# Moving two subtract/add steps from VectorE to GpSimd, and one projection in place of two, in a four-layer scan network

## The chip, the cores and the metric

The kernel runs on one NeuronCore of a Trainium2 chip. The metric is the device time of one launch in microseconds. Three runs of the kernel before gave 19587.28, 19610.84 and 19634.19 us, so the median is 19610.84 us. The engines are called as in the profile: PE (TensorE, matmuls), DVE (VectorE), ACT (ScalarE), POOL (GpSimd), and SP, which issues the DMAs. Each engine works through its own instructions in order; semaphores make one engine wait for another.

## The reference

The input is four images of 64 x 64 tokens with 96 channels, in float32. Four layers follow, each with a mixer and a feed-forward part, both with a residual. The mixer of layer 0 is a small gated recurrence. The mixers of layers 1 to 3 are selective scans over the image in four directions (row order and column order, each forward and backward), with 192 inner channels and 16 states. Cut to what matters:

```python
xz = x_norm @ in_proj_w.T;  xc, z = split(xz)          # 192 + 192
xc = silu(depthwise_conv3x3(xc) + conv_b)
xs = stack([rows, columns, flip(rows), flip(columns)]) # 4 directions
x_dbl = einsum('bkdl,kcd->bkcl', xs, x_proj_weight)    # 6 + 16 + 16 rows
dts, B, C = split(x_dbl, [6, 22])
delta = softplus(dt_w @ dts + dt_bias)
h = exp(delta * A) * h + (delta * u) * B               # along 4096 tokens
y = sum_n(h * C) + D * u
out = (layernorm(sum of directions of y) * silu(z)) @ out_proj_w.T
x = x + out
t = x + ffn(layernorm(x))      # ffn on float8-rounded values
```

The line that gives `dts`, `B` and `C` from `x_dbl`, and the residual `x = x + out`, are the two places that the change touches.

## The kernel before, in words

**Stages.** First comes `gated`, layer 0 of all images. Then `scans` runs twelve stages, one for each image of layers 1, 2 and 3. At the end the feed-forward part of the last image is left over and runs alone.

**The scan.** A stage is 2 directions of time x 4 segments of 1024 tokens x 3 channel chunks x 16 states = 384 tiles, so 4608 tiles in all. One tile is 128 partitions x 1024 tokens: two halves of 64 channels in row and column order. For tile `k`, with its state `n`:

- `c_rows`: SP reads two rows of C from a DRAM buffer `cs`, each spread over 64 partitions, into `c` (6 buffers), two tiles ahead
- `decays`: ACT makes `da = exp(delta * A)` (3 buffers), two tiles ahead
- `b_rows`: PE spreads a row of B over 128 partitions of PSUM with a selecting matmul, into `bc` (2 buffers), one tile ahead
- `scan`: DVE multiplies `bc` by `du`, then runs the recurrence into `h` (3 buffers)
- `times_c`: POOL multiplies `h` by `c`, for the tile before
- `accumulate`: PE adds `h * c` to `acc` in PSUM, for the tile three before

**Work beside the scan.** Everything else is written as Python generators that `yield` between steps. Between the multiply and the recurrence of each tile the function `beside` takes one step of `chain` (`prepare_chunk`: `delta` and `du` of the next 16 tiles), one step of `segment` (`prepare_segment`: the projections of the next 48 tiles), and some steps of a `Job`. A `Job` is the work between two mixers of one image: `join_orders`, `mixer_out`, `feed_forward`, `take_in`, `convolve`, eight strips of 512 tokens each. It earns `rate` steps a tile (1.65 for most jobs). A step is only taken when one of two PSUM banks (`bank`, `release`) is free where it needs one. The order thus written out in Python is the order on each engine, since the class `InOrder` chains the instructions of an engine. All its calls have one line in the profile, L78.

**B in three parts.** The selecting matmul works in bf16, and B is held as a sum of three bf16 numbers in the 96 partitions of `bs`: the rounded value, the rounded remainder, and the remainder of that. `prepare_segment` gets B in three copies (partitions 0 to 95) and `dts` (12 partitions) from one projection, `x_proj_b`, per half segment. ACT copies `dts` into `rows` and the rounded B into `bs`; DVE subtracts `bs` from the PSUM copy of B, into `rows`; ACT copies this to two thirds of `bs`; POOL makes the last subtraction. A second projection, `x_proj_c`, then gives the 32 rows of C, which ACT copies into `rows` and SP writes to `cs`.

**The residual.** `mixer_out` ends a strip with the projection `out_proj` into PSUM; DVE adds it to the strip `xr` of x, giving `x1` (tile `x`). One step later DVE takes the layer norm's statistics of `x1` (`measure`: `bn_stats` into `st`, `bn_aggr` into `mv`).

Of the kernel before, what the change touches and what calls it, by code (L numbers as in the profile page):

```python
# [15 lines left out]
ALU = mybir.AluOpType  # L16
# [4 lines left out]
C = 96  # L21
NS = 16
DI = 192
R = 6
HID = 4 * C
T = 1024
MM = 512
G = MM // 128
# [8 lines left out]

NB3 = 96
NC2 = 2 * NS
XPW = NB3 + 2 * R + NC2  # L40
W_IN = 0
W_OUT = W_IN + 6 * 128
W_CW = W_OUT + 2 * C
# [5 lines left out]
W_XP = W_LN + 4  # L49
W_SSM = W_XP + 6 * XPW  # L50

# [48 lines left out]
def metaformer(ctx: ExitStack, tc: tile.TileContext, x, l0_ab, l0_rest, ssm, ffn, out):  # L100
    nc = tc.nc
    pe, act, dve, pool, sp = (
        InOrder(tc, e) for e in (nc.tensor, nc.scalar, nc.vector, nc.gpsimd, nc.sync)
    )
# [6 lines left out]
    def sb(bufs, tag, shape, dtype=F32):  # L111
        return pools[bufs].tile(shape, dtype, tag=tag, name=tag)

    def const(name, shape, dtype=F32):
        return pools[1].tile(shape, dtype, name=name)
# [9 lines left out]
    def bank(name):  # L125
        banks["free"] -= 1
        return banks["pool"].tile([128, MM], F32, tag="ps", name=name)

    def release():
        banks["back"] += 1  # L130
# [31 lines left out]
    for k in range(2):  # L162
        p = slice(64 * k, 64 * k + 64)
# [31 lines left out]
    for layer in range(4):  # L195
# [8 lines left out]
        b = const(f"b_{layer}", [128, 3 + C])  # L204
# [72 lines left out]
    class Weights:  # L277
# [17 lines left out]
        def load_xp(self):  # L295
            if self.xp is None:
                self.xp = sb(1, "xp", [128, 6 * XPW])
                sp.dma_start(out=self.xp, in_=ssm[self.layer - 1, :, W_XP:W_SSM])
# [57 lines left out]
    def mixer_out(im, layer, s, hold):  # L356

        w = weights[layer].w
        yt, norm = hold.pop(("y", s))
        zl, zh, xr = load_z(im, s)  # L360
        yield from norm.settle()
        yield
        normalise(yt, yt, DI, norm.r, norm.nm)
        yield
        yield True
        g = []
        for i, (a, b, z) in enumerate(((0, 128, zl), (128, 192, zh))):
            ps = bank("y_c")
            transpose_strip(ps, yt, a, b)
            yield  # L370
            v = sb(1, f"u{i}", [128, MM])
            m = b - a
            sc, bias = (w[0:m, W_LN + 2 * i + k : W_LN + 2 * i + k + 1] for k in range(2))
            act.activation(v[0:m], ps[0:m], AF.Identity, bias=bias, scale=sc)
            release()
            yield i == 0
            g.append(v)
            if i == 0:
                continue
            for v, z, m in ((g[0], zl, 128), (g[1], zh, 64)):  # L380
                pool.tensor_tensor(v[0:m], v[0:m], z[0:m], ALU.mult)
                yield
        yield True
        ps = bank("out_proj")
        for q in range(G):
            t = slice(128 * q, 128 * q + 128)
            o = ps[:, C * q : C * q + C]
            pe.matmul(o, g[0][:, t], w[:, W_OUT : W_OUT + C], start=True, stop=False)
            pe.matmul(o, g[1][0:64, t], w[0:64, W_OUT + C : W_OUT + 2 * C], start=False, stop=True)
            yield  # L390
        yield
        x1 = sb(2, "x1", [128, G, C])
        dve.tensor_tensor(x1, xr, ps[:, 0 : G * C].rearrange("p (g c) -> p g c", g=G), ALU.add)
        release()
        yield
        norm = Norm()
        yield from norm.measure(x1, C, 1e-5)
        hold["x", s] = x1, norm
# [376 lines left out]
    def prepare_segment(item, sg):  # L775

        xp = weights[item.layer].xp
        m = NB3 + 2 * R

        def project(ps, a, b, k):  # L780

            for c in range(3):
                o = (3 * item.d + c) * XPW
                cols = slice(k * MM, (k + 1) * MM)
                pe.matmul(
                    ps[0 : b - a],
                    xp[:, o + a : o + b],
                    sg.us[c][:, cols],
                    start=c == 0,
                    stop=c == 2,  # L790
                )
                if c:
                    yield

        sg.rows = sb(1, "rows", [128, T])
        for k in range(2):
            cols = slice(k * MM, (k + 1) * MM)
            ps = bank("x_proj_b")
            yield from project(ps, 0, m, k)

            bs = sg.bs[:, cols]
            act.copy(sg.rows[NB3:m, cols], ps[NB3:m])
            sg.steps = k == 1
            act.copy(bs, ps[0:NB3])
            yield
            rem = sg.rows[0:NB3, cols]
            dve.tensor_tensor(rem, ps[0:NB3], bs, ALU.subtract)
            release()
            yield
            for p in (32, 64):  # L810
                act.copy(bs[p : p + 32], rem[p : p + 32])
            yield k == 0
        pool.tensor_tensor(sg.bs[64:96], sg.rows[64:96], sg.bs[64:96], ALU.subtract)
        for k in range(2):
            cols = slice(k * MM, (k + 1) * MM)
            yield True
            ps = bank("x_proj_c")
            yield from project(ps, m, m + NC2, k)
            act.copy(sg.rows[0:NC2, cols], ps[0:NC2])
            release()  # L820
        yield
        sp.dma_start(out=sg.cs, in_=sg.rows[0:NC2])

    def prepare_chunk(item):

# [481 lines left out]
    with tc.tile_pool(name="pbig", bufs=2, space=bass.MemoryType.PSUM) as wides_pool:  # L1307
        wides.append(wides_pool)
        with tc.tile_pool(name="pl0", bufs=1, space=bass.MemoryType.PSUM) as pl0:
            gated(images, Job(between(images[0], 0), 2.6, patience=1), pl0)  # L1310
        stages = [(im, layer) for layer in range(1, 4) for im in images]
        jobs = []
        for at in range(len(stages)):
            jobs.append([])
            if at + 1 < len(stages):
                im, layer = stages[at + 1]
                jobs[-1].append(Job(between(im, layer - 1), 1.65))

            for im in {10: images[:2], 11: images[2:3]}.get(at, ()):
                jobs[-1].append(Job(between(im, 3, im.dst), 2.6))  # L1320
        with tc.tile_pool(name="pac", bufs=1, space=bass.MemoryType.PSUM) as pac:
            scans(stages, jobs, pac)
# [38 lines left out]
def _scan(in_w, conv_w, conv_b, xp_w, dt_w, dt_b, A_logs, Ds, ln_w, ln_b, out_w):  # L1361
    w = np.zeros((128, W_SSM), np.float32)
    twice = np.r_[128:DI, 128:DI]

    xp = np.zeros((128, 2, 3, XPW), np.float32)
    m = NB3 + 2 * R
    for d in range(2):
        for chunk, halves in enumerate(CHUNKS):
            for k, (ch, order) in enumerate(halves):
                t = xp_w[2 * d + order].T[ch : ch + 64]  # L1370
                v = xp[64 * k : 64 * k + 64, d, chunk]
                for s in range(3):
                    v[:, 32 * s + NS * order : 32 * s + NS * order + NS] = t[:, R : R + NS]
                v[:, NB3 + R * order : NB3 + R * order + R] = t[:, :R]
                v[:, m + NS * order : m + NS * order + NS] = t[:, R + NS :]
    w[:, W_XP:W_SSM] = xp.reshape(128, -1)
    t = in_w.T
    w[:C, W_IN : W_IN + 448] = np.concatenate([t[:, :128], t[:, twice], t[:, DI:]], 1)
    dt = np.zeros((2 * R, 2, 3, 128), np.float32)
    for d in range(2):  # L1380
        for chunk, halves in enumerate(CHUNKS):
            for k, (ch, order) in enumerate(halves):
                t = dt_w[2 * d + order].T
                dt[R * order : R * order + R, d, chunk, 64 * k : 64 * k + 64] = t[:, ch : ch + 64]
    w[NB3 : NB3 + 2 * R, W_IN:W_OUT] = dt.reshape(2 * R, -1)
    w[:, W_OUT : W_OUT + C] = out_w.T[:128]
    w[:64, W_OUT + C : W_CW] = out_w.T[128:]
    taps = conv_w.reshape(DI, 9)
    w[:, W_CW : W_CW + 9] = taps[:128]
    w[:64, W_CW + 9 : W_CB] = np.concatenate([taps[128:, 0:3], taps[128:, 6:9]], 1)  # L1390
    w[64:, W_CW + 9 : W_CW + 12] = taps[128:, 3:6]
    w[:, W_CB:W_DTB] = np.stack([conv_b[:128], conv_b[twice]], 1)
    w[:, W_DTB:W_AL] = _chunks(dt_b[..., None]).reshape(128, -1)
    w[:, W_AL:W_DS] = _chunks(A_logs.reshape(4, DI, NS)).reshape(128, -1)
    w[:, W_DS:W_LN] = _chunks(Ds.reshape(4, DI, 1)).reshape(128, -1)
    w[:, W_LN : W_LN + 2] = np.stack([ln_w[:128], ln_b[:128]], 1)
    w[:64, W_LN + 2 : W_XP] = np.stack([ln_w[128:], ln_b[128:]], 1)
    return w
# [46 lines left out]
```

## Time and profile before

| what | value |
|---|---|
| median of the runs | 19610.84 us |
| time of the profiled execution | 19605.71 us |
| its span on the core | 19603.9 us |
| granted TensorE clock, mean | 0.816 |
| ACT busy | 62% of the span |
| DMA engines, queue q1 | 61.6% of their span |
| ACT table loads | 1165, 1494.7 us |

A page of the profile shows the busy time of each engine and the costliest groups of instructions. A group's line has the engine, the operation, the tiles written and read (out<-in), the shape, the count, the busy time and the mean duration of one, and after a bar the time that the engine stood idle just before these instructions, with what ended it. A list of waits sums the same idle time by who waited for whom. Waits under 150 ns are not put down to anyone.

### The profile page before, as it was taken

Reading aid. Unit: us, or ns where it says so; the run is one execution under the profiler, and the core shown is the slowest. Engines: PE = TensorE matmul, PEld = TensorE weight load, DVE = VectorE, ACT = ScalarE, POOL = GpSimd, SP = SyncE. Lnnn points to the kernel's source line nnn. Section 1 sums busy time; section 2 is a strip of 40 time slices with the busy share of each in tenths; the row PEclk is TensorE's granted clock in tenths of the full one; section 3 lists DMA queues with packets and bytes.
Section 4 is the critical chain, followed back from the end, with each engine's and each line's share of the span. In section 5 each row is a group of like instructions: output and inputs, shape, how many; then the busy total and the mean of one; then the engine's idle time right before and its main releaser. Section 6 shows DMA issues by size and latency. Waiting matters only on the chain. (4 is left out here: it accounts for less than half of the span.)

```text
span 19603.9 us, 224830 instructions
## 1 busy us (share of the span) xinstructions
PE 16279.3 (83%) x70400; PEld 4745.4 (24%) x70400; DVE 17669.3 (90%) x13768; ACT 12248.8 (62%) x19341; POOL 15496.4 (79%) x10086
## 2 busy tenths in 40 slices
PE   8998787787888888887888887887888888888877
PEld 3332121121122222222222222222222222223223
DVE  6757999999999999999999999999999999998885
ACT  4544665665665665675665665665675665666665
POOL 3435888888888888888888888888888888888886
PEclk9998786787787787797797797797797797797776
DMA  2213666676666666667666667666666666676664
GB/s 52 50 47 89 166 184 168 168 188 166 169 186 172 170 182 180 167 185 182 169 183 180 167 182 183 167 182 182 168 186 178 168 185 176 171 185 171 168 177 115
DMA packets 1269876, 3192.65 MB, mean 163 GB/s; under 512 B 440336, under 2 KB 440560, under 8 KB 1262544
## 3 DMA queue, kind: packets, MB, share of 16 engines
q1 hardware_dynamic: 1268688, 3178.27, 61.6%
q8 instruction: 568, 9.31, 0.2%
q14 instruction: 620, 5.08, 0.1%
HBM read 2818.81 MB, written 308.28 MB: 160 GB/s over the span
## 5 line engine op out<-in xcount | busy, mean ns | idle before, releaser
L78 POOL TENSOR_TENSOR c<-h,c 128x1024 f32<-128x1024 f32 (+1 forms) x4992 | 11332.9, 2276 | 3284.9 <-DVE h L78 1396.4
L78 DVE TENSOR_TENSOR_SCAN h<-da,carry,bc 128x1024 f32<-128x1024 f32 x4608 | 10797.5, 2343 | 598.7 <-POOL c L78 80.8
L78 PE MATMUL acc<-c,twice 64*64 64x512 f32 x36864 | 6246.6, 755 | 57.4 <-POOL c L78 57.4
L78 ACT ACTIVATE da<-delta,decay 128x1024 f32<-128x1024 f32 x4608 | 5280.8, 1148 | 1372.5 <-DVE h L78 1359.7
L78 DVE TENSOR_TENSOR bc<-du,bc 128x1024 f32<-128x1024 f32 x4608 | 5567.1, 1208 | 417.8 <-PE bc L78 389.6
L78 PE MATMUL bc<-bs,sel 96*128 96x512 bf16 x9216 | 3398.6, 457 | 2393.3 <-DVE h L78 2296.6
L78 ACT COPY carry<-h 128x1 f32<-128x1 f32 x3456 | 649.1, 188 | 2997.7 <-DVE h L78 2992.8
L78 PEld LDWEIGHTS <-sel 96*128 96x128 bf16 x9216 | 557.0, 101 | 7376.4 <-DVE h L78 5607.2
L78 PEld LDWEIGHTS acc<-c,twice 64*64 64x64 f32 x36864 | 1131.3, 153 | 2848.4 <-issue 1927.6
L78 ACT ACT_TABLE_LOAD x1165 | 1494.7, 1283 | 36.3 <-DVE mv L78 20.0
L78 PE MATMUL conv<-pad,tap_lo 128*128 128x512 f32 x1728 | 913.5, 639 | 0.6 <-ACT zh L78 0.6
L78 PE MATMUL dt_proj<-rows,w 12*128 12x512 f32 x1152 | 829.5, 807 | 6.3 <-ACT delta L78 6.3
L78 ACT ACTIVATE du<-e,ones 128x1024 f32<-128x1024 f32 x576 | 659.4, 1145 | 202.9 <-POOL delta L78 197.8
L78 POOL TENSOR_TENSOR delta<-delta,du 128x1024 f32<-128x1024 f32 x288 | 679.2, 2358 | 121.7 <-ACT du L78 121.3
L78 PE MATMUL x_proj_c<-u,xp 128*32 128x512 f32 x1152 | 657.8, 687 | 133.2 <-ACT rows L78 125.0
L78 PE MATMUL x_proj_b<-u,xp 128*108 128x512 f32 x1152 | 696.1, 722 | 53.7 <-ACT u L78 12.8
L78 ACT COPY y<-acc 128x1024 f32<-128x1024 f32 x288 | 291.3, 1012 | 713.8 <-PE acc L78 708.9
L78 POOL TENSOR_TENSOR e<-e,du 128x1024 f32<-128x1024 f32 x288 | 679.7, 2360 | 2.4 <-ACT du L78 2.4
L78 POOL TENSOR_TENSOR du<-delta,u 128x1024 f32<-128x1024 f32 x288 | 680.0, 2361 | 0.1
L78 POOL TENSOR_TENSOR delta<-delta,e 128x1024 f32<-128x1024 f32 x288 | 678.7, 2357 | 0.1
L78 ACT ACTIVATE c<-c,l_bias 128x512 f32<-128x512 f32 x384 | 263.6, 686 | 662.6 <-PE c L78 659.8
L78 PE MATMUL conv<-pad,tap_hi 128*128 128x512 f32 (+1 forms) x1152 | 598.8, 621 | 3.8 <-ACT u L78 3.8
(152 smaller groups left out, 15323.9 us busy)
## 6 DMA issues: line engine op xcount, KB each, us to landing
c<-cs SPq DMA_DIRECT2D x9216, 256.0 KB, 4.2
u<-u SPq DMA_DIRECT2D x288, 512.0 KB, 6.8
y<-y SPq DMA_DIRECT2D x1152, 128.0 KB, 3.5
y<-y SPq DMA_DIRECT2D x144, 512.0 KB, 6.4
xr<-x SPq DMA_DIRECT2D x224, 192.0 KB, 5.1
u<-u SPq DMA_DIRECT2D x288, 128.0 KB, 2.7
pad<-y SPq DMA_DIRECT2D x288, 128.0 KB, 5.1
z<-zl SPq DMA_DIRECT2D x96, 256.0 KB, 3.4
```

The costliest lines, as they stand in the source:

```text
L78: ins = f(*a, **k).ins
```

## The change

1. `prepare_segment` has one projection in place of two, over 108 output rows in a new order: B once (0 to 31), C (32 to 63), B again (64 to 95), `dts` (96 to 107). The weight columns of `xp` are laid out for it. `x_proj_c` and its copies are gone.
2. ACT copies all 108 rows into `rows`, and B rounded to bf16 into `bs[0:32]`. The first subtraction of B's parts runs on POOL, on 32 partitions, from `rows` and `bs`, both in SBUF. ACT's two copies to `bs` follow two steps later. The write of C to `cs` comes right after them, ahead of POOL's last subtraction.
3. In `mixer_out` ACT copies `out_proj` out of PSUM into `x1`, one step later POOL adds `xr` to it, and two steps after that the statistics begin.
4. Most jobs have the rate 1.62 in place of 1.65.

```diff
-XPW = NB3 + 2 * R + NC2
+XPW = NB3 + 2 * R
...
         x1 = sb(2, "x1", [128, G, C])
-        dve.tensor_tensor(x1, xr, ps[:, 0 : G * C].rearrange("p (g c) -> p g c", g=G), ALU.add)
+        act.copy(x1, ps[:, 0 : G * C].rearrange("p (g c) -> p g c", g=G))
         release()
+        yield
+        pool.tensor_tensor(x1, x1, xr, ALU.add)
+        yield
         yield
         norm = Norm()
...
     def prepare_segment(item, sg):
         xp = weights[item.layer].xp
+        rows = sg.rows = sb(1, "rows", [128, T])
+        for k in range(2):
+            cols = slice(k * MM, (k + 1) * MM)
+            ps = bank("x_proj")
             for c in range(3):
                 o = (3 * item.d + c) * XPW
                 pe.matmul(
+                    ps[0:XPW], xp[:, o : o + XPW], sg.us[c][:, cols], start=c == 0, stop=c == 2
                 )
                 if c:
                     yield
             bs = sg.bs[:, cols]
-            act.copy(sg.rows[NB3:m, cols], ps[NB3:m])
+            act.copy(rows[0:XPW, cols], ps[0:XPW])
             sg.steps = k == 1
-            act.copy(bs, ps[0:NB3])
-            yield
-            rem = sg.rows[0:NB3, cols]
-            dve.tensor_tensor(rem, ps[0:NB3], bs, ALU.subtract)
+            act.copy(bs[0:32], ps[0:32])
             release()
             yield
+            rem = rows[64:96, cols]
+            pool.tensor_tensor(rem, rows[0:32, cols], bs[0:32], ALU.subtract)
+            yield
+            yield
             for p in (32, 64):
-                act.copy(bs[p : p + 32], rem[p : p + 32])
+                act.copy(bs[p : p + 32], rem)
             yield k == 0
-        pool.tensor_tensor(sg.bs[64:96], sg.rows[64:96], sg.bs[64:96], ALU.subtract)
-        for k in range(2):
-            cols = slice(k * MM, (k + 1) * MM)
-            yield True
-            ps = bank("x_proj_c")
-            yield from project(ps, m, m + NC2, k)
-            act.copy(sg.rows[0:NC2, cols], ps[0:NC2])
-            release()
-        yield
-        sp.dma_start(out=sg.cs, in_=sg.rows[0:NC2])
+        sp.dma_start(out=sg.cs, in_=rows[NC2 : 2 * NC2])
+        pool.tensor_tensor(sg.bs[64:96], rows[64:96], sg.bs[64:96], ALU.subtract)
...
-                jobs[-1].append(Job(between(im, layer - 1), 1.65))
+                jobs[-1].append(Job(between(im, layer - 1), 1.62))
```

More of the change, by code (lines that the diff above doesn't have):

```diff
@@ L777, in prepare_segment @@
         xp = weights[item.layer].xp
-        m = NB3 + 2 * R
-        def project(ps, a, b, k):
+        rows = sg.rows = sb(1, "rows", [128, T])
+        for k in range(2):
+            cols = slice(k * MM, (k + 1) * MM)
+            ps = bank("x_proj")
             for c in range(3):
                 o = (3 * item.d + c) * XPW
-                cols = slice(k * MM, (k + 1) * MM)
                 pe.matmul(
[L786 to L790, printed above, removed]
+                    ps[0:XPW], xp[:, o : o + XPW], sg.us[c][:, cols], start=c == 0, stop=c == 2
                 )
@@ L793, in project @@
                     yield
-        sg.rows = sb(1, "rows", [128, T])
-        for k in range(2):
-            cols = slice(k * MM, (k + 1) * MM)
-            ps = bank("x_proj_b")
-            yield from project(ps, 0, m, k)
             bs = sg.bs[:, cols]
-            act.copy(sg.rows[NB3:m, cols], ps[NB3:m])
+            act.copy(rows[0:XPW, cols], ps[0:XPW])
             sg.steps = k == 1
-            act.copy(bs, ps[0:NB3])
-            yield
-            rem = sg.rows[0:NB3, cols]
-            dve.tensor_tensor(rem, ps[0:NB3], bs, ALU.subtract)
+            act.copy(bs[0:32], ps[0:32])
             release()
             yield
+            rem = rows[64:96, cols]
+            pool.tensor_tensor(rem, rows[0:32, cols], bs[0:32], ALU.subtract)
+            yield
+            yield
             for p in (32, 64):
-                act.copy(bs[p : p + 32], rem[p : p + 32])
+                act.copy(bs[p : p + 32], rem)
             yield k == 0
-        pool.tensor_tensor(sg.bs[64:96], sg.rows[64:96], sg.bs[64:96], ALU.subtract)
-        for k in range(2):
-            cols = slice(k * MM, (k + 1) * MM)
-            yield True
-            ps = bank("x_proj_c")
-            yield from project(ps, m, m + NC2, k)
-            act.copy(sg.rows[0:NC2, cols], ps[0:NC2])
-            release()
-        yield
-        sp.dma_start(out=sg.cs, in_=sg.rows[0:NC2])
+        sp.dma_start(out=sg.cs, in_=rows[NC2 : 2 * NC2])
+        pool.tensor_tensor(sg.bs[64:96], rows[64:96], sg.bs[64:96], ALU.subtract)
     def prepare_chunk(item):
@@ L1365, in _scan @@
     xp = np.zeros((128, 2, 3, XPW), np.float32)
-    m = NB3 + 2 * R
     for d in range(2):
@@ L1371, in _scan @@
                 v = xp[64 * k : 64 * k + 64, d, chunk]
-                for s in range(3):
-                    v[:, 32 * s + NS * order : 32 * s + NS * order + NS] = t[:, R : R + NS]
+                v[:, NS * order : NS * order + NS] = t[:, R : R + NS]
+                v[:, NC2 + NS * order : NC2 + NS * order + NS] = t[:, R + NS :]
                 v[:, NB3 + R * order : NB3 + R * order + R] = t[:, :R]
-                v[:, m + NS * order : m + NS * order + NS] = t[:, R + NS :]
     w[:, W_XP:W_SSM] = xp.reshape(128, -1)
```

## The prediction

> **What bounds the kernel now.** I read the busy times first, then the same by stretch. In a stretch's row come its length, then each engine's busy time.
>
> ```profile
> PE 16279.3 (83%) x70400; PEld 4745.4 (24%) x70400; DVE 17669.3 (90%) x13768; ACT 12248.8 (62%) x19341; POOL 15496.4 (79%) x10086
> ```
> ```profile
> core 0: us, PE busy (x) PEld busy (x) DVE busy (x) ACT busy (x) POOL busy (x), PEclk, DMA share, GB/s
> ...
> 2700.00:18900.00 16200.00, 13428.88 (x60392) 3721.43 (x60390) 15179.46 (x10951) 10425.05 (x15995) 13570.31 (x8024) 0.81 0.67 176
> ```
>
> The scans fill 1804 to 19388 us. In their middle DVE is busy 15179 of 16200 us (94%), POOL 84%, PE 83%. DVE is the bound, with 1021 us of gaps. The groups of instructions by shape price DVE's work, removed rows last:
>
> ```profile
> L78 DVE TENSOR_TENSOR_SCAN h<-da,carry,bc 128x1024 f32<-128x1024 f32 x4608 | 10797.5, 2343 | 598.7 <-POOL c L78 80.8 <-ACT norm L78 20.7 <-ACT da L78 5.4
> L78 DVE TENSOR_TENSOR bc<-du,bc 128x1024 f32<-128x1024 f32 x4608 | 5567.1, 1208 | 417.8 <-PE bc L78 389.6 <-POOL carry L78 23.3 <-PE ff_xt L78 2.7
> L78 DVE TENSOR_TENSOR rows<-x_proj_b,bs 96x512 f32<-96x512 f32 x192 | 130.1, 677 | 45.5 <-ACT bs L78 45.3
> L78 DVE TENSOR_TENSOR x<-xr,out_proj 128x384 f32<-128x384 f32 x96 | 52.6, 548 | 70.9 <-PE out_proj L78 46.6 <-issue 14.7 <-POOL hq L78 9.2
> ```
>
> The change takes 130.1 + 52.6 = 182.7 us of busy time off DVE. The timeline of DVE shows that this is not the gain (start, duration):
>
> ```profile
> 4074.82 2.35 DVE L78 TENSOR_TENSOR_SCAN h<-da,carry,bc 128x1024 f32<-128x1024 f32 x1
> 4077.09 1.21 DVE L78 TENSOR_TENSOR bc<-du,bc 128x1024 f32<-128x1024 f32 x1
> 4078.43 2.35 DVE L78 TENSOR_TENSOR_SCAN h<-da,carry,bc 128x1024 f32<-128x1024 f32 x1
> 4080.69 1.21 DVE L78 TENSOR_TENSOR bc<-du,bc 128x1024 f32<-128x1024 f32 x1
> 4081.81 0.68 DVE L78 TENSOR_TENSOR rows<-x_proj_b,bs 96x512 f32<-96x512 f32 x1
> 4082.40 2.33 DVE L78 TENSOR_TENSOR_SCAN h<-da,carry,bc 128x1024 f32<-128x1024 f32 x1
> ```
>
> From `h` to `h` a bare tile takes 4078.43 - 4074.82 = 3.61 us, a tile with the subtraction 4082.40 - 4078.43 = 3.97. The scan needs the multiply's result and in the bare tile starts 0.13 us after its end; an instruction between them fills that gap, and overlaps both neighbours by 0.09 us. So 0.68 us of work costs 0.37.
>
> **What the Trainium skill says, and the trace.** "Perfetto Trace Analysis", section Optimizing Scalar/DVE Operations, says that part of a DVE instruction's latency, its write acknowledgement, overlaps with the next instruction; the 0.09 us above agrees. "GPSIMD Engine Reference", section Elementwise, has a two-input operation run about twice as long on GpSimd as on DVE; here 128x1024 takes 2360 ns on POOL, and 1208 ns on DVE with one input in PSUM. "PSUM — Partial Sum Buffer", section Specifications, gives GpSimd no access to PSUM; hence ACT's copies, and no POOL row here has a PSUM input. "SBUF — State Buffer", section Who interferes with whom, warns that a DVE `tensor_tensor` with both inputs in SBUF contends with GpSimd's reads. Here every frequent one reads one input from PSUM, and the recurrence varies little (2303 to 2355 ns), so I charge DVE nothing for busier POOL ports.
>
> **The change part by part.** The sum is made against the profiled execution, 19605.7 us (span 19603.9), 5 us under the median of 19610.8.
>
> *A, DVE instructions gone.* Of 192 subtractions 190 lie between scan tiles. Counted in the trace, 167 stand alone between multiply and recurrence; the median such tile without a wait takes 3.976 us against 3.604 for a bare one: 167 x 0.372 = 62 us. The other 23 have neighbours; they cost 0.68 - 0.09 = 0.59 each: 14 us. Of the 96 adds 8 fall after the scan; 40 stand alone (3.840 - 3.604 = 0.236 each, 9 us) and 48 have neighbours (0.46 to 0.59, 25 us). Sum **-110 us**.
>
> *B, their own waits.* The adds wait for `out_proj` and the subtractions for `bs`: between scan tiles 31.0 and 27.8 us. ACT takes these waits over; its `da` runs two tiles ahead and itself waited 1360 us for DVE. **-59 us**, bounds -20 to -65.
>
> *C, PE relieved.* 1152 matmul passes of `x_proj_c` at about 0.57 us of busy time (657.8 us) leave PE; the remaining projection costs what `x_proj_b` did, 108 columns either way. In the middle of the scans DVE waits thus:
>
> ```profile
> DVE bc L78 <- PE bc L78: 347.8, 247, 5.0
> DVE h L78 <- POOL c L78: 80.8, 36, 12.5
> DVE x L78 <- PE out_proj L78: 27.4, 18, 2.9
> DVE rows L78 <- ACT bs L78: 26.2, 14, 2.8
> DVE st L78 <- ACT yt L78: 23.3, 18, 2.6
> ```
>
> The first line is PE late with `bc` because something long stands before it in its queue. By position among the 48 tiles of a segment, counted over the whole trace, 172 of its 389.6 us fall on tiles 2 to 8 of the third chunk, where `x_proj_c` runs; the other 41 positions have 5.3 us each, so 172 - 37 = 135 us are in excess. Sharing each wait out over the extra matmuls of the 7.4 us before it gives `x_proj_c` 105. I take **-120**, bounds -50 (other job matmuls move into the place) to -170.
>
> *D, POOL's added work and the waits for it.* 192 subtractions of 32x512: half of POOL's own 32x1024 one (2124 ns), 1.06 us, 204 us in all. 96 adds of 128x384 at about 0.95 (0.915 with one f16 input): 91. So 295 us on an engine with 2115 us of idle before `c` in the middle alone, 1289 of them for `h` of DVE. It counts only where POOL is late. Counted in the trace, `c` ends 2.5 us after its `h` in half of the tiles, more than 3.9 after it in 30%, more than 7.5 in 5%. The statistics of `x1` come in the tile after POOL's add for 64 strips and two tiles after it for 24 (program order). One tile on, DVE gets there about 4.8 us after that `h`'s end; with 0.95 for the add it waits where the lag exceeds 3.85: 30% of tiles, say 40% with other job work beside it, some 1.3 us each: 64 x 0.4 x 1.3 = 33. Beyond that, a late `c` holds back `h` (80.8 us now); 288 instructions of about 1 us, 5 to 7% of them where POOL is already near three tiles late, add 17. **+50**, bounds +10 to +130. ACT's copies of the remainder stand two tiles behind the subtraction, so `da`, `carry` and PSUM copies queued behind them wait only in the 5% tail: nothing. If POOL were later there, `da` would be late next.
>
> *E, the tail.* After the last tile eight strips go one after another with DVE 17% busy. DVE's 0.55 us becomes ACT 0.47 + POOL 0.95, with a longer hand-over: about 1 us a strip if nothing covers it. **+8**, bounds 0 to +16.
>
> *F, at nothing.* ACT loses 192 copies of 560 ns and gains 96 of about 470, beside DVE. SP has as many DMAs as before (13185); the write of `cs` comes five to seven tiles earlier and is not waited for at its own place. Rate 1.62: in program order the main jobs end at tile 339 to 344 of 384, before at 336 to 344, and the forced finish is at 356, so no burst. POOL's last subtraction moves one or two tiles later, its result being needed 13 tiles on.
>
> Sum: -110 - 59 - 120 + 50 + 8 = -231, so 19605.7 - 231 = **19375 us**. The bounds give -335 (19271) and -34 (19572).
>
> **Rivals.** *POOL becomes the bound (slower).* If every added POOL instruction pushes DVE back by its full length, because POOL is already three tiles of `h` behind where it comes, that is +295 us, and with no relief on PE: -110 - 59 + 295 + 8 = +134, 19740 us. It decides from about 0.6 us lost per added instruction (177 / 288) without C. For it speaks that `c` lags by 5 us or more in 15% of tiles, bunched where a chunk is prepared (four 2.36 us instructions). Against: DVE waits only 81 us for `c` now, POOL waits 1289 us for DVE, and the subtractions come at chunk ends, away from that bunch. *The relief on PE is lost:* C = 0 and D at 100 us give -61, 19545 us. For it: PE's clock is throttled to 0.81 and jobs fill freed steps; against, the waits stand where `x_proj_c` stands. *PE's relief is larger:* bank waits of PE go too (`x_proj_c` for `rows` of ACT, 283 us on PE and its weight loads), and C reaches 250: -361, 19245 us.
>
> **How the numbers follow.** The forecast has 0.62, lost relief 0.16 (a third of it within 0.2%), the larger relief 0.13, POOL as the bound 0.09 (a little of it within 0.2%). 0.2%, 39 us, is about what a measurement of this kernel tells from no change. Faster 0.86, same 0.06, slower 0.08. The range 19260 to 19570 takes the bounds of the sum and nearly reaches the larger relief; it leaves out POOL as the bound.
>
> **What would show it.** Right: no DVE rows for `rows` and `x`; bare tiles still 3.60 us; waits of `bc` for PE near 270; a new wait of `st` for POOL `x` of 20 to 50 us; `h` for POOL `c` near 100; POOL up by 295 us. Wrong: `bc` for PE unchanged (C), `h` or `st` for POOL over 200 us (D), the scan's mean duration changed (ports), or DVE waiting for `da`.

## The result, and the profile after

The changed kernel takes 19522.49 us (median), the kernel before in the same comparison 19615.54: a ratio of 0.9957, 95% interval 0.9944 to 0.9970. So the change gains some 93 us of the 231 forecast. The profiled execution took 19515.9 us, with a span of 19514.1.

The busy times by engine, from the page of the changed kernel:

```profile
PE 16029.3 (82%) x69248; PEld 4684.7 (24%) x69248; DVE 17525.9 (90%) x13480; ACT 12143.3 (62%) x19240; POOL 15800.4 (81%) x10374
```

DVE has the 288 instructions fewer and is busy 143 us less. POOL is busy 304 us more, close to the forecast's 295. PE lost 1152 passes, worth 657.8 us before, but its busy time fell by 250 us only. The groups of instructions of the changed kernel tell why, on PE first, and then what was added on POOL:

```profile
L78 PE MATMUL acc<-c,twice 64*64 64x512 f32 x36864 | 6432.9, 776 | 51.7 <-POOL c L78 48.5 <-DMA y<-y 3.1
L78 PE MATMUL bc<-bs,sel 96*128 96x512 bf16 x9216 | 3512.6, 471 | 2530.6 <-DVE h L78 2438.9 <-DMA c<-cs 65.0 <-DMA y<-y 12.6
L78 POOL TENSOR_TENSOR rows<-rows,bs 32x512 f32<-32x512 f32 x192 | 220.8, 1150 | 35.0 <-ACT bs L78 20.2
L78 POOL TENSOR_TENSOR x<-x,xr 128x384 f32<-128x384 f32 x96 | 95.8, 998 | 31.6 <-ACT x L78 31.6
```

The same 36864 `acc` matmuls took 755 ns each before and take 776 now; `bc` went from 457 to 471. Their busy time grew by 186 and 114 us, so 300 us of PE's relief came back as slower matmuls. The ends of matmuls are modelled in the profile, but the starts say the same: the two matmuls of one `bc` start 291 ns apart on average, before 281 (counted in the traces). The granted clock, a mean over the span, fell from 0.816 to 0.794. The added POOL instructions measure 1.15 and 1.00 us (1.06 and 0.95 were assumed). DVE's recurrence takes 2343 ns as before, so the busier POOL did not slow it.

DVE's waits, whole trace:

```profile
DVE bc L78 <- PE bc L78: 358.5, 243, 6.1
...
DVE st L78 <- POOL x L78: 164.4, 62, 9.0
...
DVE h L78 <- POOL c L78: 85.1, 42, 13.3
...
DVE h L78 <- ACT da L78: 32.7, 38, 2.6
```

The first line stood at 389.6 before. The second is new: 108.7 us of it in 54 waits between scan tiles, the other 55.7 in the part after the scan. The third is unchanged. The last was 5.4.

One of these new waits, in the timeline of DVE and then in that of POOL for the same stretch (start, duration):

```profile
8189.67 1.21 DVE L78 TENSOR_TENSOR bc<-du,bc 128x1024 f32<-128x1024 f32 x1
8190.79 0.41 DVE L78 BATCH_NORM_STATS2 st<-xh 128x6 f32<-128x96 f32 x2
8193.96 0.42 DVE L78 BATCH_NORM_STATS2 st<-x 128x6 f32<-128x96 f32 x2 [2.76 <-POOL x L78]
```
```profile
8185.14 2.35 POOL L78 TENSOR_TENSOR c<-h,c 128x1024 f32<-128x1024 f32 x1
8187.46 2.34 POOL L78 TENSOR_TENSOR du<-delta,u 128x1024 f32<-128x1024 f32 x1
8189.77 0.91 POOL L78 TENSOR_TENSOR xh<-x,ff_y 128x384 f32<-128x384 f32 x1
8190.64 2.33 POOL L78 TENSOR_TENSOR c<-h,c 128x1024 f32<-128x1024 f32 x1
8192.94 0.98 POOL L78 TENSOR_TENSOR x<-x,xr 128x384 f32<-128x384 f32 x1
```

DVE stands still for 2.76 us behind an add of 0.98 us, since POOL has a chunk's `du`, another strip's `xh` and the product for the last tile in front of it. The recurrence of the next tile is queued behind the waiting `st`.

Against the forecast's steps, between the two profiled executions (span 19603.9 to 19514.1, so -90):

| step | forecast | seen |
|---|---|---|
| A: DVE's instructions | -110 | not contradicted: rows gone, bare tile 3.603 us (3.604 before) |
| B: their own waits | -59 | gone from DVE; `h` for `da` of ACT +27 in their place |
| C: PE relieved | -120 | `bc` for PE: -31 |
| D: waits for POOL | +50 | `st` for `x` +109, `h` for `c` +4 |
| E: after the scan | +8 | 216.1 to 233.6 us: +17 |
| F: nothing | 0 | smaller waits between tiles, `norm`, `yt`, `xh` and others: -41; start of the scan -4 |

With A taken as forecast, the right column adds up to -88.

### The profile page after: what moved, and what is told of

The parts are those of the page before. It is cut to its first block, busy times and chain, and to the rows that moved or that the text cites. A ratio compares the mean times of both kernels' runs of the same rounds, so it can differ in the third digit from the quotient of the medians.

```text
span 19514.1 us, 222410 instructions
## 1 busy us (share of the span) xinstructions
PE 16029.3 (82%) x69248; PEld 4684.7 (24%) x69248; DVE 17525.9 (90%) x13480; ACT 12143.3 (62%) x19240; POOL 15800.4 (81%) x10374
## 5 line engine op out<-in xcount | busy, mean ns | idle before, releaser
L78 DVE TENSOR_TENSOR_SCAN h<-da,carry,bc 128x1024 f32<-128x1024 f32 x4608 | 10798.0, 2343 | 636.5 <-POOL c L78 84.5
L78 PE MATMUL acc<-c,twice 64*64 64x512 f32 x36864 | 6432.9, 776 | 51.7 <-POOL c L78 48.5
L78 PE MATMUL bc<-bs,sel 96*128 96x512 bf16 x9216 | 3512.6, 471 | 2530.6 <-DVE h L78 2438.9
L78 PE MATMUL x_proj<-u,xp 128*108 128x512 f32 x1152 | 711.6, 736 | 59.5 <-DMA xp<-in_ssm 15.5
L78 DVE TENSOR_TENSOR_SCAN h<-da,l_carry,bc 128x512 f32<-128x512 f32 x384 | 491.4, 1280 | 42.5 <-DVE bc L78 1.8
```

The source lines that it names most:

```text
L78: ins = f(*a, **k).ins
```

## The experiments

Twelve kernels ran, each timed in turn with the kernel before (19621 to 19631 us). Ratios are to the kernel before, with 95% intervals. The changed kernel stands at 0.9957 with jobs' rate 1.62. A difference of two medians is good to some 20 us; taken from the ratios instead, the differences below come out up to 28 us apart, and the larger ones have both figures. Each trace is of one execution, often the slowest of its run, so the waits are compared with the spans of the traces. The edits are shown shortened.

**1. The residual add back on DVE.**

```diff
-        act.copy(x1, ps[...])
-        release(); yield
-        pool.tensor_tensor(x1, x1, xr, ALU.add)
-        yield; yield
+        dve.tensor_tensor(x1, xr, ps[...], ALU.add)
+        release(); yield
```

> The changed kernel with the residual add put back on DVE, reading out_proj from PSUM, one step before the statistics; the one projection and the subtraction on POOL stay. Theory (the hand-over of x1 from POOL is what ate the gain): the waits of st for POOL x go (109 us between scan tiles, 56 in the tail), the adds come back with 34 us and their waits for out_proj with about 31 + 15: time 19522 - 165 + 34 + 46 = 19437, give or take 25; in the last scan stage some 20 us faster than the changed kernel, in the tail 10 to 18. Rival (those waits only stand where DVE would wait for something else anyway): 19500 to 19530, no faster than the changed kernel.

Measured: 19393.34 us, 0.9887 (0.9873 to 0.9900), below what the theory allowed. Without the move of the residual add the change gains 228 us; with it, 93. Its waits on DVE:

```profile
DVE bc L78 <- PE bc L78: 309.9, 229, 6.5
...
DVE h L78 <- POOL c L78: 79.8, 32, 14.4
...
DVE x L78 <- PE out_proj L78: 52.0, 27, 7.4
```

`st` no longer waits for POOL `x`; the adds' waits for `out_proj` are back at 52; and `bc` waits for PE 49 us less than in the changed kernel. Between the two spans lie 107 us. Between scan tiles the changed kernel has +109 of `st` and +49 of `bc`, and saves the adds' 34 and 36 of their waits; after the scan it takes 18.6 us more (215.0 to 233.6): 107 in sum. The 49 of `bc` are what the theory did not have. That PE is later where ACT empties `out_proj` is seen; how it comes about was not tried.

**2. The residual add alone moved.** The same lines the other way round, in the kernel before, rate 1.65.

> The kernel before with the residual add alone moved: ACT copies, POOL adds, statistics two steps later; projections and rate as before. Theory: removes 34 us of DVE and 46 of waits, brings 165 of waits of st for POOL x: 19615 + 85 = 19700, slower than before by 0.2 to 0.6%. Rival (moving the add pays by itself, as the prediction had it with 34 + 31 gained, 33 to 50 lost): 19590 to 19620.

Measured: 19736.10 us, 1.0058 (1.0045 to 1.0071), slower as the theory has it, but not by its waits:

```profile
DVE bc L78 <- PE bc L78: 573.3, 359, 18.6
...
DVE st L78 <- POOL x L78: 87.3, 28, 11.7
```

Between tiles `st` waits only 22 us for POOL, while `bc` waits 184 us more for PE. In program order the main jobs now end at tile 352 to 355 of 384 (336 to 344 before), and in two stages they run into the forced finish at 356. How much of the 184 us that makes, and how much the later emptying of PSUM, stays open.

**3. PE's work put back.** Matmuls like those of the second projection, in the old steps, into PSUM that nobody reads, rate 1.65.

```diff
         pool.tensor_tensor(sg.bs[64:96], rows[64:96], sg.bs[64:96], ALU.subtract)
+        for k in range(2):
+            yield True
+            ps = bank("again")
+            ...  (3 matmuls of 32 rows each, yields as in the first projection)
+            release()
-                jobs[-1].append(Job(between(im, layer - 1), 1.62))
+                jobs[-1].append(Job(between(im, layer - 1), 1.65))
```

> The changed kernel with the matmuls of the second projection (32 rows of C, 1152 passes) done again in the old place into a PSUM bank that nobody reads; no copy of ACT follows; rate 1.65. Theory (PE's granted clock follows its work, so taking matmuls off PE gave a lower clock and most of the time came back): the mean granted clock rises from 0.794 to about 0.815, acc matmuls fall from 776 to about 755 ns and bc from 471 to 457, waits of bc for PE stay within 340 to 400 us, time 19522 to 19570. Rival (the clock is another matter, and relief was small because the job's matmuls make these waits): clock stays 0.79, PE busy rises by the full 650 us, waits of bc for PE rise by 100 us or more, time 19620 or over.

Measured: 19473.07 us, 0.9927 (0.9914 to 0.9939), faster than the changed kernel, which no theory had. Clock 0.809, `acc` 757 ns, `bc` for PE 406.6. Two edits had been made in one run; the next tells them apart.

**4. Statistics two steps later.** Two more `yield`s after POOL's add.

> The changed kernel with two more steps between POOL's add and the statistics of x1, so that they stand two or three tiles on in place of one or two. Theory: POOL is late by one tile at most in most cases, so waits of st for POOL x between scan tiles fall from 109 to under 30 us and the time to about 19440; the tail is unchanged or a few us longer. Rival (POOL's queue as a whole is late and DVE waits for it at the next place): waits of h for POOL c rise from 85 by as much, time within 20 us of 19522.

Measured: 19424.92 us, 0.9904 (0.9889 to 0.9920). Two of its waits on DVE:

```profile
DVE h L78 <- POOL c L78: 75.1, 30, 11.4
...
DVE st L78 <- POOL x L78: 55.9, 10, 9.6
```

Of the second line 54.4 us lie after the scan and 1.5 between tiles. The time is the theory's. So it is a hand-over fetched too early, not POOL's throughput: POOL does the same work here.

**5. The rate alone.** 1.62 back to 1.65 in the changed kernel.

> The changed kernel with the jobs' rate back at 1.65. Two readings of the run with PE's work put back (19473, which had rate 1.65 too) are told apart. If the rate made it faster: 19460 to 19490 here. If PE's extra work did, by its higher clock: 19510 to 19535 here, clock 0.794 as in the changed kernel.

Measured: 19423.50 us, 0.9895 (0.9882 to 0.9909). That is faster than either reading had it. The 1.8% fewer job steps a tile, costed at nothing in the forecast, cost 99 us here (122 by the ratios). The waits on DVE:

```profile
DVE bc L78 <- PE bc L78: 347.1, 262, 8.5
...
DVE st L78 <- ACT yt L78: 96.9, 31, 32.9
DVE st L78 <- POOL x L78: 94.6, 33, 8.9
```

Of the 94.6 us 53.8 lie after the scan; between tiles 40.8 are left of 108.7. In program order both rates have 56 strips of the main stages 35 to 21 at one and two tiles between add and statistics; what differs is where in a chunk of 16 tiles the adds fall. At 1.62, 43 of 88 adds end 7 us or more after the `h` of the `c` product in front of them, at 1.65 29 do (counted in the traces). DVE comes for the result 4.8 us after that `h` where it comes one tile later. That count alone does not order the runs: at rate 1.68 (11) it is 29 too, but the waits are 77 us, and in 3 it is 42 with waits of 57. Why a rate places the adds well or badly stays open. Between the two spans lie 73 us: these waits give 68, `h` for `da` 20 and `bc` 11, and a later start of the scan and smaller waits take some back.

Set against this run, putting PE's matmuls back (3), without ACT's copies that followed them, costs 50 us (63 by the ratios).

**6. PE's work doubled in place.** Every matmul of the one projection twice in the same step, rate 1.62.

```diff
-                pe.matmul(ps[0:XPW], ..., start=c == 0, stop=c == 2)
+                for again in range(2):
+                    pe.matmul(ps[0:XPW], ..., start=c == 0 and again == 0, stop=c == 2 and again == 1)
```

> The changed kernel with every matmul of the one projection issued twice in the same step, accumulating (so B, C and dts come out twice as large): 1152 more passes of about 0.6 us on PE, steps, rate and all other instructions as in the changed kernel. Theory (PE's clock follows its work and gives most of the time back): mean granted clock 0.81 to 0.82, acc matmuls about 755 to 760 ns, waits of bc for PE between 330 and 440 us, time 19500 to 19570. Rival (clock independent, PE's added time is simply late for bc): clock 0.79, waits of bc for PE over 460 us, 19620 or more.

Measured: 19597.27 us, 0.9983 (0.9976 to 0.9991), 75 us over the changed kernel (51 by the ratios). Groups on PE, then the wait:

```profile
L78 PE MATMUL acc<-c,twice 64*64 64x512 f32 x36864 | 6351.7, 766 | 51.2 <-POOL c L78 51.2
L78 PE MATMUL bc<-bs,sel 96*128 96x512 bf16 x9216 | 3474.7, 466 | 2398.3 <-DVE h L78 2308.5 <-DMA c<-cs 73.2 <-DMA y<-y 3.7
L78 PE MATMUL x_proj<-u,xp 128*108 128x512 f32 x2304 | 1210.0, 667 | 46.2 <-DMA xp<-in_ssm 11.6 <-ACT u L78 10.4 <-ACT hq L78 9.5
```
```profile
DVE bc L78 <- PE bc L78: 470.6, 339, 6.1
```

More matmuls made the others faster: `acc` 776 to 766 ns, `bc` 471 to 466, clock 0.794 to 0.805, with nothing else changed in the program but these matmuls and their results. The starts of a `bc`'s two matmuls lie 287 ns apart, 291 in the changed kernel. PE's busy time rose by 326 us for 498 more in `x_proj`. But the wait rose by 112 us, which is the difference of the two spans (115). Both theories are half right: the clock follows the work, and the work still costs time. Taking such matmuls off PE is worth 50 to 75 us.

**7. Later statistics, and DVE's add after the scan.** Experiment 4, with a flag set when the scan is over.

```diff
+        if alone[0]:
+            dve.tensor_tensor(x1, xr, part, ALU.add); release(); yield
+        else:
             act.copy(x1, part); release(); yield
             pool.tensor_tensor(x1, x1, xr, ALU.add)
+            for _ in range(4): yield
```

> The changed kernel with the statistics two steps later, and in the last image's part after the scan the add on DVE as before. Theory (in the tail the hand-over ACT to POOL to DVE lies on the path, 18 us; between scan tiles POOL's add costs nothing when DVE comes for it late enough): tail of 216 us in place of 236, time 19425 - 20 = 19405. Rival (the tail is bound elsewhere): 19425.

Measured: 19385.38 us, 0.9873 (0.9860 to 0.9887). The part after the last recurrence takes 215 us (235.8 in 4). The theory holds, and it is faster than the changed kernel by 137 us (165 by the ratios).

**8. One projection, both small operations on DVE.** Experiment 1, and the subtraction on DVE from PSUM, with one step fewer after it.

```diff
-            release(); yield
-            pool.tensor_tensor(rem, rows[0:32, cols], bs[0:32], ALU.subtract)
-            yield; yield
+            yield
+            dve.tensor_tensor(rem, ps[0:32], bs[0:32], ALU.subtract)
+            release(); yield
```

> One projection in place of two, but both small operations on DVE, reading PSUM as before (the first subtraction on 32 partitions). Against the run with the residual add alone put back (19393). Theory (each subtraction costs DVE 0.37 us between multiply and recurrence, 76 us in all, and some 28 us of waits; POOL does it free): 19393 + 76 + 28 - 25 for da waits that go = 19470, give or take 25. Rival (all of the gain comes from the merged projection): 19380 to 19410.

Measured: 19482.25 us, 0.9924 (0.9911 to 0.9936). The merged projection, with the rate 1.62, gains 149 us, the subtraction's move to POOL another 89 (73 by the ratios), as the theory has it. DVE's row for the subtraction, and its wait for PE:

```profile
L78 DVE TENSOR_TENSOR rows<-x_proj,bs 32x512 f32<-32x512 f32 x192 | 131.0, 682 | 72.0 <-ACT bs L78 66.9
```
```profile
DVE bc L78 <- PE bc L78: 282.3, 218, 6.1
```

On a third of the partitions the subtraction takes DVE as long (682 against 677 ns). `bc` waits 107 us less for PE than in the kernel before. In the changed kernel the subtraction's results are fetched two tiles later by ACT, not by DVE.

**9 to 12. Rates.** Experiment 1 at 1.65; the changed kernel at 1.59 and 1.68; experiment 7 at 1.65.

> The residual add back on DVE (as in the run at 19393 with rate 1.62), now with rate 1.65. Theory (the rate matters by where the strips' adds fall in POOL's queue, and only through DVE's waits for them): no such wait here, so no effect of the rate: 19375 to 19415. Rival (1.62 lines all the job's work up worse with the scan, on PE and ACT too): 19290 to 19340.

> The changed kernel with rate 1.59. Theory: by program order 49 of 56 strips of the main stages have the statistics one tile after POOL's add (35 at 1.62 and 1.65), so waits of st for POOL x between scan tiles stay near 100 us or rise to 130: 19500 to 19560. Rival (time falls steadily with the rate's distance from 1.62, or rises steadily as the rate falls): 19420 or 19620.

> The changed kernel with rate 1.68: 28 strips of the main stages at one tile, 28 at two. Theory: waits of st for POOL x 30 to 60 us between scan tiles, as at 1.65: 19400 to 19450. Rival (1.65 was a lucky case and most rates are like 1.62): 19500 to 19550.

> Statistics two steps later, DVE's add in the tail (19385 at rate 1.62), now with rate 1.65. Theory: the waits of st for POOL x were gone already, so the rate changes little: 19365 to 19405. Rival (the rate's gain of 99 us is of another kind and adds up): 19290 to 19330.

| kernel | rate | time | ratio (interval) | `st` for POOL `x` between tiles |
|---|---|---|---|---|
| add on DVE (1) | 1.62 | 19393.34 | 0.9887 (0.9873 to 0.9900) | none |
| add on DVE (9) | 1.65 | 19378.42 | 0.9876 (0.9863 to 0.9889) | none |
| changed (10) | 1.59 | 19499.73 | 0.9940 (0.9928 to 0.9951) | 98 |
| changed | 1.62 | 19522.49 | 0.9957 (0.9944 to 0.9970) | 109 |
| changed (5) | 1.65 | 19423.50 | 0.9895 (0.9882 to 0.9909) | 41 |
| changed (11) | 1.68 | 19499.42 | 0.9942 (0.9928 to 0.9955) | 77 |
| later statistics, DVE tail (7) | 1.62 | 19385.38 | 0.9873 (0.9860 to 0.9887) | 1 |
| later statistics, DVE tail (12) | 1.65 | 19411.65 | 0.9897 (0.9884 to 0.9911) | 3 |

Without an early fetch from POOL, 1.65 in place of 1.62 moves the time by 15 us down (1 to 9) and 26 up (7 to 12), 22 and 47 by the ratios; with it, by 99 down (122). So most of the rate's effect goes through that fetch, as the theory of 9 and 12 has it, though 12 is 7 us above what it allowed. At 1.68 the theory was wrong: the waits were expected at 30 to 60 us. 1.65 is the favourable case among four rates, and no rule for it was found. The fastest kernels are 9, 7 and 1, which their intervals don't separate.

So even with the fetch put right, moving the residual add gains nothing over leaving it on DVE: 7 against 1 is 8 us faster, 12 against 9 is 33 slower. In 7 and 12 `bc` waits 47 and 61 us more for PE than in 1 and 9, which takes up most or all of what DVE saves (some 34 for the adds by the forecast's prices, and their waits, 36 at 1.62 and 12 at 1.65).

## Why the prediction was right or wrong

The direction and the range held. The size did not: -231 forecast, about -93 measured.

Experiments 8 and 1 split the change into three parts, and the forecast's terms can be sorted into the same parts:

| part | forecast | by medians | by ratios |
|---|---|---|---|
| one projection, rate 1.62 (before to 8) | C: -120 | -149 | -149 |
| subtraction to POOL (8 to 1) | A -76, B -28, D +17: -87 | -89 | -73 |
| residual add to ACT and POOL (1 to changed) | A -34, B -31, D +33, E +8: -24 | +129 | +137 |

The medians add up to -109 and the ratios to -85, since the kernel before itself moved by some 15 us between comparisons. Two parts came out near the forecast, and the third takes the whole miss.

**A held, as far as it was tried.** Costing a removed instruction by the tile with it less the tile without it, 0.37 us in place of 0.68, fits the second part. The adds' share was not tried alone.

**D was mis-sized, and is the main failure.** It priced the wait for the residual add at 33 us: POOL's add right behind a `c` product, and 40% of 64 strips waiting 1.3 us. In the trace 54 of 88 waited, 2.0 us each, 109 us in all. The add ends on average 6.6 us after the `h` of that product, not 3.5: the product itself ends 4.6 us after its `h` at these places (the forecast had 2.5 in half of all tiles; the median before is 3.0), and in half of the cases other POOL work of the same job steps comes between, 1.0 us on average over all. The price of the residual's move, 129 us at 1.62 (changed against 1) and 45 at 1.65 (5 against 9), also includes PE's later `bc`, which no step had.

**F was wrong on the rate.** The forecast looked for a burst of job steps, found none, and put the rate at nothing. With the early fetch of D it was worth 99 us.

**C was right in kind, but lost 49 us to something it left out.** Where DVE keeps the residual add, `bc` waits 282 to 310 us for PE (8, 9, 1), near the forecast's 270. Where ACT and POOL have it, it waits 347 to 368 (changed, 4, 5, 7, 10, 11, 12), whatever the rate and the place of the statistics. So the residual's new route brings the waits of `bc` back; whether by ACT's later emptying of `out_proj`, by the two or more added job steps a strip, or otherwise, stays open. By place, the waits where `x_proj_c` stood fell from 172 us to 95 (50 in experiment 1), while those at all other places rose from 218 to 264 (259). The sum also took the clock as given: PE's clock fell with its work, and the matmuls alone are worth 50 to 75 us (3 and 6); the rest of the first part's 149 us was not divided further.

**B held on DVE, but** ACT's `da` was costed at nothing: 27 us more at 1.62. At 1.65 `h` waits 12.5 us for it in experiment 5, but 21 in 9 and 28 in 12 (5.4 before), so it hangs on the place of the steps too.

**E** was 17 us for 8: eight strips, 2.2 us each. Experiment 7 shows that the hand-over is the cause.

**The rivals.** POOL did not become the bound: `h` waits for `c` as before (experiment 4 has POOL do all of its new work at 19425). The relief on PE was lost in part, as the second rival had it: to the residual's new route, to the clock, and to waits at other places.

**Slips in the forecast's figures.** The first rival's break-even adds E's 8 us where it should take it off: 161 us and not 177, 0.56 us per instruction. DVE is busy 14% of the time after the last tile (29.75 of 216 us), not 17%. Neither changes the sum.

## What to carry to other kernels

An operation moved to an engine with idle time is paid for at the place where its result is fetched: read how late that engine's queue is there, with everything issued ahead of the operation, and move the fetch back before judging the move. Then ask what the new route does to the engines that it passes: here it made PE late, and the move gained nothing even with the fetch put right. Where work is interleaved by a rate, treat the rate as part of the change and time the change at several; here it made the same move cost 45 or 129 us. Take a removed instruction's worth from neighbouring tiles with and without it, not from its own duration.

## What the runs showed of the hardware that was not expected

In this kernel PE's granted clock goes up with PE's work. In the traces, all ten kernels without the extra matmuls had a mean of 0.788 to 0.796, the four with them (the kernel before, 2, 3 and 6) 0.805 to 0.816. By stretch of the kernel before, it is 0.93 in the first 1790 us, where PE is busy 88% of the time, 0.81 in the scans at 83%, and 0.51 after the scan at 75%; these stretches differ in their matmuls too. The Trainium skill gives a reason in "TensorE: Matmul & The Clock Gate", section What's actually happening: the clock is gated by how busy PE has been of late. Experiment 6 agrees: 1152 passes more took 10 ns off each `acc` matmul.
